# Two layers on one core: where the first loads stand, and how the last three groups' expert tiles are strung together

## The chip, the core and the metric

The kernel runs on one core of a Trainium2 chip, in one launch. The core has TensorE (PE in the profile; its weight loads are PEld), VectorE (DVE), ScalarE (ACT), GpSimd (POOL) and SyncE (SP). Each works through its own queue of instructions in order. DMA transfers are issued from the queues of SP, ACT and POOL. The metric is the device time of one execution in microseconds (us); the median of several runs counts.

## What is computed

Eight sequences of 1024 tokens with 256 channels pass four residual blocks, each `x = x + layernorm(block(layernorm(x)))`: differential attention with 16 heads, a feed-forward block with ternary weights, a gated convolution of 15 taps, and a mixture of 16 experts of which each token takes two.

```python
x = L0_attn_x                                    # (8, 1024, 256)
x = x + _layernorm(_L0_attn_ref(_layernorm(x), ...))
x = x + _layernorm(_L0_ffn_ref(_layernorm(x), ...))
x = x + _layernorm(_L1_attn_ref(_layernorm(x), ...))     # the convolution
x = x + _layernorm(_L1_ffn_ref(_layernorm(x), ...))      # the experts

# attention: two softmax maps per head, the second taken off with a factor lam
lam = exp(sum(lq1 * lk1)) - exp(sum(lq2 * lk2)) + LAM_INIT
comb = a1 - lam[None, :, None, None] * a2
# experts
weights, idx = _gate(xf, gate_w, gate_b)         # two of 16 per token, by groups
h = silu(xf @ We1[e] + be1[e]) * (xf @ We3[e] + be3[e])
y = sum over the two of weights * (h @ We2[e] + be2[e])
z = silu(xf @ ws1 + bs1) * (xf @ ws3 + bs3) @ ws2 + bs2   # for every token
return y + z
```

All of it is in float32.

## The kernel before

Attention (0 to some 2600 us) is an order written out by hand. Time is counted in steps `t` of the pipeline; ten steps make one pair of heads, and `plan` says which helper moves on at which step. The first step is -52, the first score of a maximum comes at step -14 (`LEAD` is 14), the first exponential at step 0. Before any of it stands a setup: the identity, the causal mask and its two halves (`parts`, four copies on SP, L219), the projection weights (loaded on ACT's queue, regrouped by VectorE, L241), WV with each head's mean taken off (L254 to L256), the lam terms (L284 to L296) and 48 rows of biases that TensorE turns into columns (`bias_columns`, L309 to L314). Then each half of a sequence is loaded (`xa`, L340), normalised (L348 to L356), turned by TensorE (L372) and copied to SBUF by ScalarE (L375). Values (L383), keys and queries (L406) follow; a key or query is copied twice by ScalarE and its rest is taken by VectorE (L411 to L414), and SP lays its rows out for the scores (L432). Until the first score these turned tiles and projections share a single PSUM buffer, `pm`.

After the feed-forward block comes the last part, also in an order by hand. For each sequence b there is a convolution (`conv(b)`) and then `gates(b)`: normalisation, the choice of two experts for each token and the shared expert `z`, which goes to DRAM. The sequences form five groups for the experts: groups 0, 1 and 2 of two sequences, groups 3 and 4 of one (sequences 6 and 7). For each group:

- `route` (24 steps with two sequences, 16 with one) counts tokens by expert and gives every token its place in tiles of 128 rows, each tile of one expert. It is mostly VectorE, with some TensorE.
- `expert_tiles` goes through the tiles, 47 for two sequences and 31 for one. In step i it does `outer` of tile i, `tile_product` of i+1, `inner` of i+2, `turn` of i+3, then fetches the weights of tile i+4 (SP, 385 KB, four buffers, L1688) and gathers the tokens of tile i+6 (POOL, an indirect DMA, three buffers, L1676). `turn` is TensorE and ScalarE, `inner` eight TensorE products and two activations (L1708 to L1716), `tile_product` one VectorE product (L1724), `outer` two TensorE products, a copy to one of two `ty` buffers and its store (L1730 to L1733).
- `collected` goes through the group's blocks of 128 tokens: `collect` gathers each token's two expert rows (POOL, `gy`, two buffers each, L1753), loads `z` (`gz`), weights and adds them on VectorE in the next step (L1764), takes the statistics (L1768, L1770), then the power on POOL (L96, L98), then normalises, adds and stores (L1774 to L1777).

`weave` runs several such streams at once: each has a number of steps, and always the one that is least far in proportion moves on. Slot b holds `conv(b)`, `gates(b-1)` and what `slots[b]` names. The part from slot 7 on, with its times in the profile, is:

| stage | us from the start | what is woven |
|---|---|---|
| slot 7 | 3657 to 3784 | conv(7), gates(6), collect of group 1, route(2) and 15 steps of group 2's tiles |
| slot 8 | 3784 to 3905 | gates(7), route(3), the other 38 steps of group 2's tiles |
| group 3 | 3905 to 4025 | 37 steps of its tiles, route(4), collect of group 2 |
| group 4 | 4025 to 4119 | 37 steps of its tiles, collect of group 3 |
| the end | 4119 to 4156 | collect of group 4 |

Of the kernel before, what the change touches and what calls it, by code (L numbers as in the profile page):

```python
# [20 lines left out]
P = 128  # L21
# [6 lines left out]
def kernel(  # L28
# [175 lines left out]
    with ExitStack() as L:  # L204
# [8 lines left out]
        whole = p2.tile([P, 2, P], F32, tag="e", bufs=4, name="whole")  # L213
        make_causal_mask(nc, whole[:, 0, :], mask_val=NEG)
        nc.vector.tensor_copy(whole[:, 1, :], ident)
        parts_ = p2.tile([P, 2, 2, P], F32, tag="e", bufs=4, name="parts")
        for r in range(2):
            for k in range(2):
                nc.sync.dma_start(  # L219
                    parts_[64 * r : 64 * r + 64, :, k, :], whole[64 * k : 64 * k + 64, :, :]  # L220
                )
        masks = wp.tile([P, 2, 2, P], F32R, name="masks")
        nc.vector.tensor_copy(masks, parts_)
# [4 lines left out]
        def pm_tile(name):  # L228
            return ps_m.tile([P, 512], F32, tag="pm", name=name)
# [5 lines left out]
        for m, (wq, wk) in enumerate(((Wq1, Wk1), (Wq2, Wk2))):  # L235
            for w, dst, s in ((wq, WQ, scale), (wk, WK, 1.0)):
                stage = p2.tile([P, ND, D], F32, tag="e", bufs=4, name="stage")
                nc.scalar.dma_start(stage, w.rearrange("(c p) e -> p c e", p=P))
                for dc in range(ND):
                    for hh in range(2):  # L240
                        nc.vector.tensor_scalar_mul(  # L241
                            dst[:, dc, :, :, 2 * hh + m, :].rearrange("p a q d -> p (a q) d"),
                            stage[:, dc, :].rearrange("p (c h d) -> p c h d", h=2, d=HD)[
                                :, :, hh, :
                            ],
                            s,
                        )


        WV = r1.tile([P, ND, H, VD], F32, name="WV")  # L250
        nc.scalar.dma_start(WV.rearrange("p c h v -> p c (h v)"), Wv.rearrange("(c p) e -> p c e", p=P))
        for dc in range(ND):
            vm = small.tile([P, H], F32, tag="hvar", name="vm")
            nc.vector.tensor_reduce(vm, WV[:, dc, :, :], AX.X, ALU.add)  # L254
            nc.vector.tensor_scalar_mul(vm, vm, 1.0 / VD)
            nc.vector.tensor_tensor(  # L256
                WV[:, dc, :, :], WV[:, dc, :, :],
                vm.unsqueeze(2).to_broadcast([P, H, VD]), ALU.subtract,
            )
        WO = q1.tile([P, NHC, D], F32, name="WO")  # L260
        nc.scalar.dma_start(WO, Wo.rearrange("(c p) e -> p c e", p=P))

# [3 lines left out]
        for p in range(2):  # L266
            mine = small.tile([P, 1], F32, tag="mine", name="mine")
            nc.vector.tensor_reduce(
                mine, ident.rearrange("p (h w) -> p h w", h=2)[:, :, 2 * p : 2 * p + 2], AX.XY,
                ALU.add,  # L270
            )
            nc.vector.tensor_scalar(chosen[:, p, :], ones, mine, None, ALU.mult)
            nc.vector.tensor_scalar(
                Ms[p].rearrange("p (n q) -> p n q", q=P),
                ones.unsqueeze(1).to_broadcast([P, NB, P]), 0.0, None, ALU.mult,
            )


        lam_e = []
        for n, (lq, lk) in enumerate(((lq1, lk1), (lq2, lk2))):  # L280
            a = q2.tile([P, H, HD], F32, tag="w2", name="lama")
            c = q2.tile([P, H, HD], F32, tag="w2", name="lamb")
            for t, src in ((a, lq), (c, lk)):
                nc.sync.dma_start(  # L284
                    t.rearrange("p h d -> p (h d)"),
                    src.rearrange("h d -> (h d)").partition_broadcast(P),
                )
            nc.vector.tensor_mul(a, a, c)
            s = p1.tile([P, H], F32, tag="lams", name="lams")
            nc.vector.tensor_reduce(s, a, AX.X, ALU.add)  # L290
            e = p1.tile([P, H], F32, tag=f"lame{n}", name="lame")
            nc.scalar.activation(e, s, AF.Exp)
            lam_e.append(e)
        nlam = const.tile([P, H], F32, name="nlam")
        nc.vector.tensor_sub(nlam, lam_e[1], lam_e[0])
        nc.vector.tensor_scalar_add(nlam, nlam, -LAM_INIT)  # L296

        def bias_columns():
            rows = q2.tile([nrow, P], F32, tag="w2", name="brows")
            at = 0  # L300
            for name, ap in (
                ("f1", fb1.rearrange("(r p) -> r p", p=P)),
                ("c1", cb1.rearrange("(r p) -> r p", p=P)),
                ("e1", be1), ("e3", be3),
                ("s1", bs1.rearrange("(r p) -> r p", p=P)),
                ("s3", bs3.rearrange("(r p) -> r p", p=P)),
            ):
                n = ap.shape[0]
                nc.sync.dma_start(rows[at : at + n, :], ap)  # L309
                col[name] = at  # L310
                at += n
            pt = pm_tile("pt")
            nc.tensor.transpose(pt[:, :nrow], rows, ident[:nrow, :nrow])
            nc.vector.tensor_copy(biasT, pt[:, :nrow])  # L314

# [597 lines left out]
        free_at = total - 2 * NS_ + 2  # L913
        with tc.manual_schedule():
            bias_columns()
            for t in range(min(plan), total + 6):
                if t == free_at:
                    right[1].close()
                    f1 = on_right(2, "ffn_1", 1)

                    F1T = f1.tile([P, ND, FF], F32R, name="F1T")
                    F2T = f1.tile([P, NF, D], F32R, name="F2T")
                    nc.sync.dma_start(F1T.bitcast(F32), f1d)
                    nc.sync.dma_start(F2T.bitcast(F32), f2d)
                step(t)
# [251 lines left out]
    with ExitStack() as L:  # L1177
# [494 lines left out]

        def fetch_tokens(g, i):
            G = groups[g]
            xs = p1.tile([P, D], F32, tag="xs", bufs=3, name="xs")
            nc.gpsimd.indirect_dma_start(  # L1676
                out=xs, out_offset=None, in_=xnd[g],
                in_offset=bass.IndirectOffsetOnAxis(ap=G["token"][:, i : i + 1], axis=0),
                bounds_check=G["blocks"] * P - 1, oob_is_err=False,
            )  # L1680
            tiles[g, i] = [xs]

        def fetch_weights(g, i):
            wt = p1.tile([P, wall.shape[2]], F32, tag="wt", bufs=4, name="wt")
# [50 lines left out]
        def expert_tiles(g):  # L1735
            LT = 2 * groups[g]["blocks"] + E - 1
            stages = (
                (0, outer), (1, tile_product), (2, inner), (3, turn),
                (4, fetch_weights), (6, fetch_tokens),
            )  # L1740
            for i in range(-6, LT):
                for d, stage in stages:
                    if 0 <= i + d < LT:
                        stage(g, i + d)
                yield

        def collect(g, n):

            G = groups[g]
            rows = []  # L1750
            for r in range(2):
                y = p1.tile([P, D], F32, tag=f"gy{r}", bufs=2, name="gy")
# [6 lines left out]
            z = p1.tile([P, D], F32, tag="gz", bufs=4, name="gz")  # L1759
            b, nb = spans[g][0] + n // NB, n % NB  # L1760
            nc.sync.dma_start(z, zd[b * T + nb * P : b * T + (nb + 1) * P, :])
            yield
            for r in range(2):
                nc.vector.scalar_tensor_tensor(  # L1764
                    z, rows[r], G["w"][r][:, n : n + 1], z, ALU.mult, ALU.add
                )
# [12 lines left out]
        def collected(g):  # L1779
# [3 lines left out]
            for k in range(NGB + 3):  # L1783
                for n in range(k - 3, k + 1):
# [23 lines left out]

        def count_route(g):
            return 9 + 8 * spans[g][1]  # L1810

        with tc.manual_schedule():
# [5 lines left out]
            for g, (b0, n) in enumerate(spans[:-2]):  # L1818
                it = chain(lambda g=g: route(g, groups[g]), lambda g=g: expert_tiles(g))
                half = (count_route(g) + count_tiles(g) + 1) // 2  # L1820
                slots[b0 + n + 1].append((it, half))
                slots[b0 + n + 2].append((it, half + 1))
                if b0 + n + 3 <= B:
                    slots[b0 + n + 3].append((later_(collected, g), n * NB + 3))
            for b in range(B + 1):
                streams = []
                after = conv_norm(b + 1) if b + 1 < B else iter(())
                if b < B:
                    streams.append((conv(b, after), 2 * len(windows) + 14))
                if b > 0:  # L1830
                    streams.append((gates(b - 1), 38))
                if b == B:
                    streams.append((later_(route, G0 - 2), count_route(G0 - 2)))
# [3 lines left out]
            weave(  # L1837
                (expert_tiles(G0 - 2), count_tiles(G0 - 2)),
                (route(G0 - 1, groups[G0 - 1]), count_route(G0 - 1)),
                (collected(G0 - 3), spans[G0 - 3][1] * NB + 3),  # L1840
            )
            weave(
                (expert_tiles(G0 - 1), count_tiles(G0 - 1)),
                (collected(G0 - 2), spans[G0 - 2][1] * NB + 3),
            )
# [49 lines left out]
```

## Time and profile before

| what | value |
|---|---|
| median of three runs | 4165.53 us (4164.99 to 4168.62) |
| the profiled execution | 4157.51 us |
| its span, first to last instruction | 4155.8 us |
| mean granted TensorE clock | 0.966 |
| busy: PE, DVE, ACT, POOL | 3770.3, 2820.1, 2307.0, 1475.0 us |

The profile shows the span in 40 equal slices of some 104 us; each digit is the busy share in tenths (PEclk: the granted clock; DMA: the mean share of the 16 DMA engines):

```profile
PE   5998999999999999999999999789999988988764
DVE  5776877876876876886786786688556357374333
ACT  2665666666665665665666666556433543534433
POOL 0222522522431432432342342544311335344465
PEclk9999999999999999999999999899999999999878
DMA  2223232232332233232232222300001655637787
```

The feed-forward block fills slices 26 to 28, the convolutions begin in slice 29, and expert tiles run from slice 32 on.

### The profile page before, as it was taken

The numbers are of one execution on the slowest core, as the hardware profiler recorded it, in microseconds if no ns is written. First come the engines' busy times: TensorE is split into PE (matmuls) and PEld (weight loads), VectorE is DVE, ScalarE is ACT, GpSimd is POOL, SyncE is SP. The second block draws the span as 40 slices with busy tenths as digits, with TensorE's granted clock in tenths as the row PEclk, the third lists the DMA queues.
The fourth block names the chain that finished last, engine by engine and source line by source line (L and its number), as shares of the span: only waits on it lengthen the run. The fifth ranks groups of instructions, "written<-read, shape, count | busy, mean of one in ns | idle before, by whom it ended". The sixth has DMA issues, their size and how long they took to land.

```text
span 4155.8 us, 81449 instructions
## 1 busy us (share of the span) xinstructions
PE 3770.3 (91%) x28903; PEld 2338.5 (56%) x28903; DVE 2820.1 (68%) x6122; ACT 2307.0 (56%) x3870; POOL 1475.0 (35%) x2500
## 2 busy tenths in 40 slices
PE   5998999999999999999999999789999988988764
PEld 2554555554554554554554555578666766766553
DVE  5776877876876876886786786688556357374333
ACT  2665666666665665665666666556433543534433
POOL 0222522522431432432342342544311335344465
PEclk9999999999999999999999999899999999999878
DMA  2223232232332233232232222300001655637787
GB/s 83 65 68 66 68 90 54 69 90 58 75 83 65 66 81 75 57 84 59 61 81 62 70 65 65 106 24 1 6 26 43 185 153 162 185 119 225 213 244 220
DMA packets 286023, 381.38 MB, mean 92 GB/s; under 512 B 61362, under 2 KB 182547, under 8 KB 285364
## 3 DMA queue, kind: packets, MB, share of 16 engines
q1 hardware_dynamic: 226964, 292.74, 26.0%
q0 software_dynamic: 16256, 44.23, 3.9%
q10 hardware_dynamic: 42400, 39.21, 3.1%
q8 instruction: 232, 3.80, 0.4%
q14 instruction: 171, 1.40, 0.1%
HBM read 175.00 MB, written 70.66 MB: 59 GB/s over the span
## 4 chain that ended last, share of the span: by engine, by line
PE 64%; DVE 10%; SPq 8%; DMA 7%; ACT 4%; issue 4%; POOL 2%; ACTq 0%; POOLq 0%; DVEq 0%
PE acc L788 10%; PE sc L751 9%; PE sc L705 6%; SPq L432 6%; PE sc L759 5%; PE pq L406 5%; PE ph L1708 3%; PE pv L383 3%; PE ph L1532 2%; ACT e L766 2%; PE ph L1297 2%; DMA wt<-wall 2%; PE ya L515 2%; PE sc L695 2%; PE py L1085 2%
## 5 line engine op out<-in xcount | busy, mean ns | idle before, releaser
L766 ACT ACTIVATE e<-sc 128x1024 f32<-128x1024 f32 (+1 forms) x1280 | 1194.5, 939 | 554.3 <-PE sc L759 524.4
L723 DVE TENSOR_REDUCE nmx<-sc 128x2 f32<-128x1024 f32 (+3 forms) x1280 | 1108.2, 900 | 343.1 <-PE sc L705 337.4
L769 POOL TENSOR_SCALAR_AFFINE_SELECT e<-e 128x256 f32<-128x256 f32 x1024 | 409.9, 414 | 873.8 <-ACT e L766 865.7
L751 PEld LDWEIGHTS sc<-Q,K 64*128 64x128 f32 x3072 | 288.9, 184 | 682.0 <-issue 490.3
L751 PE MATMUL sc<-Q,K 64*128 64x512 f32 (+3 forms) x3072 | 649.8, 428 | 25.1 <-DVE nmx L723 20.6
L788 PE MATMUL acc<-e,V 128*32 128x512 f32 (+3 forms) x6144 | 631.3, 497 | 0.1
L759 PE MATMUL sc<-M,chosen 64*128 64x512 f32 (+3 forms) x3072 | 531.6, 342 | 11.5 <-DMA M<-mt 11.5
L705 PE MATMUL sc<-K,Q 64*128 64x128 f32 (+3 forms) x4608 | 510.9, 300 | 22.0 <-ACT e L766 15.8
L715 DVE TENSOR_REDUCE nmx<-sc 128x8 f32<-128x1024 f32 x256 | 313.2, 1224 | 204.3 <-PE sc L705 201.5
L705 PEld LDWEIGHTS sc<-K,Q 64*128 64x128 f32 x4608 | 366.8, 186 | 101.7 <-ACT e L766 58.0
L98 POOL TENSOR_TENSOR rstd<-ve,nhalf 128x1 f32<-128x1 f32 (+3 forms) x352 | 394.8, 1121 | 29.3
L1676 POOL DMA_INDIRECT xs<-xnd,r_token x203 | 209.6, 1032 | 346.0 <-PE pt L1695 275.8
L822 POOL TENSOR_TENSOR O<-op 128x124 f32<-128x124 f32 x256 | 123.5, 503 | 563.5 <-DVE op L817 530.1
L1708 PE MATMUL ph<-xT,wt 128*128 128x128 f32 x1624 | 245.0, 298 | 83.6 <-DMA wt<-wall 50.0
L759 PEld LDWEIGHTS sc<-M,chosen 64*128 64x128 f32 x3072 | 293.6, 187 | 13.2 <-DMA M<-mt 11.8
L1708 PEld LDWEIGHTS ph<-xT,wt 128*128 128x128 f32 x1624 | 221.9, 206 | 135.3 <-ACT xT L1699 58.1
L1724 DVE TENSOR_TENSOR thT<-th 128x128 f32<-128x128 f32 x203 | 58.4, 290 | 244.7 <-ACT th L1716 220.9
L788 PEld LDWEIGHTS acc<-e,V 128*32 128x32 f32 x6144 | 130.0, 108 | 131.2 <-issue 81.6
L96 POOL TENSOR_SCALAR ve<-armv 128x1 f32<-128x1 f32 (+1 forms) x224 | 57.4, 256 | 347.4 <-DVE armv L1344 151.5
L1713 ACT ACTIVATE th<-ph,wt 128x128 f32<-128x128 f32 x203 | 74.6, 368 | 180.1 <-PE ph L1708 127.6
L411 ACT COPY raw<-pq 128x512 f32<-128x512 f32 (+1 forms) x160 | 80.2, 501 | 161.4 <-PE pq L406 145.3
L1753 POOL DMA_INDIRECT gy<-yd,r_posu x128 | 134.7, 1052 | 83.6 <-DMA yd<-ty 47.9
(276 smaller groups left out, 6378.3 us busy)
## 6 DMA issues: line engine op xcount, KB each, us to landing
wt<-wall SPq DMA_DIRECT2D x203, 385.0 KB
K<-KC SPq DMA_DIRECT2D x1024, 64.0 KB
Q<-QC SPq DMA_DIRECT2D x1024, 64.0 KB
yd<-ty ACTq DMA_DIRECT2D x203, 128.0 KB
xa<-in_L_attn_x_dram SPq DMA_DIRECT2D x16, 512.0 KB
M<-mt SPq DMA_DIRECT2D x512, 4.0 KB
xr<-in_L_attn_x_dram SPq DMA_DIRECT2D x64, 128.0 KB
x<-xr SPq DMA_DIRECT2D x64, 128.0 KB
```

The lines of the kernel that those rows point to most:

```text
L98: nc.gpsimd.tensor_tensor(rstd, ve, nhalf[:, :n], ALU.pow)
L432: nc.sync.dma_start(d[:, s, :], src[rows, half, :].bitcast(F32))
L705: nc.tensor.matmul(sc[:, r, at_ : at_ + w], quad["Q", i // GB][rows, p, (i % GB) * P : (i % GB + 1) * P], quad["K", k0 // TG][rows, p, k0 ...
L715: nc.vector.tensor_reduce(maxima[b, c][0][:, maps, i : i + GB], sc.rearrange("p m (n q) -> p m n q", q=P), AX.X, ALU.max, negate=True,)
L723: nc.vector.tensor_reduce(maxima[b, c][k][:, maps, i if k == 1 else i - GB], sc[:, :, at_ : at_ + w], AX.X, ALU.max, negate=True,)
L751: nc.tensor.matmul(sc[:, r, at_ : at_ + w], quad["K", kb // GB][rows, p, (kb % GB) * P : (kb % GB + 1) * P], quad["Q", g][rows, p, q0:], s ...
L759: nc.tensor.matmul(sc[:, r, at_ : at_ + w], chosen[rows, p, :], quad["M"][rows, qs], start=False, stop=True,)
L766: nc.scalar.activation(e[:, :, :cols], sc[:, :, :cols], AF.Exp)
L769: nc.gpsimd.affine_select(out=sq, in_=sq, compare_op=ALU.is_ge, fill=0.0, base=0, pattern=[[0, 2], [1, P]], channel_multiplier=-1,)
L788: nc.tensor.matmul(acc[32 * r : 32 * r + 32, q0:], Vs[b, kb][:, 2 * c + r // 2, :], es[r // 2][:, r % 2, at_ : at_ + TG - q0], start=(kb = ...
L1676: nc.gpsimd.indirect_dma_start(out=xs, out_offset=None, in_=xnd[g], in_offset=bass.IndirectOffsetOnAxis(ap=G["token"][:, i : i + 1], axis= ...
L1708: nc.tensor.matmul(ph[:, m, :P], wt[:, k : k + P], xT[:, dc * P : (dc + 1) * P], start=(dc == 0), stop=(dc == ND - 1),)
```

## The change

Two parts of the kernel change. At the start, the setup is cut into helpers (`lay_masks`, `attention_weights`, `bias_columns`) that `plan` places among the first steps. The load of xa comes first on SP; weights, masks and lam terms are loaded on ACT's queue, the bias rows at step 0. While `t` is below -14, turned tiles and projections take the three score buffers (`sc`) instead of the one `pm`.

In the last part, the tiles of groups 2, 3 and 4 become one sequence of 109 tiles that begins in slot 7 (24 steps of route(2), then 31 of tiles) and runs on through six weaves; slot 8 is gone. For groups 3 and 4 the weights are fetched six tiles ahead into eight buffers and the tokens eight ahead into eight, the new ones cut from the tiles of sequences 0 to 3, which are done by then (`more_buffers`). The collects of groups 2, 3 and 4 have four `gy` and five `gz` buffers and one step more between the gather and its use.

```diff
         masks = wp.tile([P, 2, 2, P], F32R, name="masks")
-        nc.vector.tensor_copy(masks, parts_)
+        def lay_masks():
+            whole = p2.tile([P, 2, P], F32, tag="e", bufs=4, name="whole")
+            make_causal_mask(nc, whole[:, 0, :], mask_val=NEG)
+            nc.gpsimd.tensor_copy(whole[:, 1, :], ident)
+            parts_ = p2.tile([P, 2, 2, P], F32, tag="e", bufs=4, name="parts")
+            for r in range(2):
+                for k in range(2):
+                    nc.scalar.dma_start(
+                        parts_[64 * r : 64 * r + 64, :, k, :], whole[64 * k : 64 * k + 64, :, :]
+                    )
+            yield
+            nc.vector.tensor_copy(masks, parts_)
+            yield
         def pm_tile(name):
+            if now[0] < -LEAD:
+                return ps_s.tile([P, 2, 512], F32, tag="sc", name="sc")[:, 0, :]
             return ps_m.tile([P, 512], F32, tag="pm", name=name)
+        def attention_weights():
+            nc.scalar.dma_start(
+                WV.rearrange("p c h v -> p c (h v)"), Wv.rearrange("(c p) e -> p c e", p=P)
+            )
...
+            for m, ws in enumerate(((Wk1, Wk2), (Wq1, Wq2))):
+                for w in ws:
+                    stage = p2.tile([P, ND, D], F32, tag="e", bufs=4, name="stage")
+                    nc.scalar.dma_start(stage, w.rearrange("(c p) e -> p c e", p=P))
+                    stages.append(stage)
+            nc.scalar.dma_start(WO, Wo.rearrange("(c p) e -> p c e", p=P))
+            yield
...
+            a, c = (q2.tile([P, 2, H, HD], F32, tag="w2", name="lam") for _ in range(2))
+            for t, srcs in ((a, (lq1, lq2)), (c, (lk1, lk2))):
+                for k, src in enumerate(srcs):
+                    nc.scalar.dma_start(
+                        t[:, k, :, :].rearrange("p h d -> p (h d)"),
+                        src.rearrange("h d -> (h d)").partition_broadcast(P),
+                    )
+            yield
             nc.vector.tensor_mul(a, a, c)
...
+        first = min(plan)
+        prepared = attention_weights()
+        spread(prepared, [(0, s) for s in (first, first + 3, first + 11, first + 12, first + 20, first + 22)])
+        at(0, first + 28, prepared)
+        spread(lay_masks(), [(0, first + 14), (0, first + 18)])
+        spread(bias_columns(), [(0, 0), (0, 3)])
         with tc.manual_schedule():
-            bias_columns()
-            for t in range(min(plan), total + 6):
+            for t in range(first, total + 6):
...
+        def more_buffers():
+            x = [xpool.tile([P, NB * D], F32, tag=f"x{k}", name=f"spare{k}") for k in range(4)]
+            w = wall.shape[2]
+            spare["wt"] = [x[k][:, j * w : (j + 1) * w] for k in (2, 3) for j in range(2)]
+            spare["xs"] = [x[k][:, 2 * w : 2 * w + D] for k in (2, 3)] + [
+                x[1][:, j * D : (j + 1) * D] for j in range(5, NB)
+            ]
+            spare["gz"] = [x[1][:, j * D : (j + 1) * D] for j in range(5)]
+            spare["gy"] = [
+                [x[0][:, (4 * r + j) * D : (4 * r + j + 1) * D] for j in range(4)]
+                for r in range(2)
+            ]
...
-        def expert_tiles(g):
...
+        def expert_tiles(*gs):
+            line = [(g, i) for g in gs for i in range(2 * groups_blocks(g) + E - 1)]
+            ahead = {g: (4, 6) if g < len(spans) - 2 else (6, 8) for g in gs}
+            w = x = 0
+            for i in range(-ahead[gs[0]][1], len(line)):
+                for d, stage in ((0, outer), (1, tile_product), (2, inner), (3, turn)):
+                    if 0 <= i + d < len(line):
+                        stage(*line[i + d])
+                while w < len(line) and w <= i + ahead[line[w][0]][0]:
+                    fetch_weights(*line[w])
+                    w += 1
+                while x < len(line) and x <= i + ahead[line[x][0]][1]:
+                    fetch_tokens(*line[x])
+                    x += 1
                 yield
...
             yield
+            if late:
+                yield
             for r in range(2):
                 nc.vector.scalar_tensor_tensor(
...
+                gs = (g,) if g < G0 - 3 else (g, g + 1, g + 2)
...
+                if g < G0 - 3:
+                    slots[b0 + n + 1].append((it, half))
+                    slots[b0 + n + 2].append((it, half + 1))
+                else:
+                    slots[b0 + n + 1].append((it, count_route(g) + LT(g) - 17))
...
+            gated_, last = gates(B - 1), later_(collected, G0 - 3)
+            weave((it, 14), (gated_, 19), (route(G0 - 2, groups[G0 - 2]), count_route(G0 - 2)))
+            more_buffers()
+            weave((it, 10), (gated_, 9))
+            weave((it, 12), (gated_, 11), (last, 10))
+            weave((it, LT(G0 - 2) - 22), (later_(route, G0 - 1), count_route(G0 - 1)), (last, 10))
+            weave((it, 11))
+            weave((it, LT(G0 - 1)), (later_(collected, G0 - 2), groups_blocks(G0 - 2) + 4))
             for _ in collected(G0 - 1):
                 pass
```

## The prediction

> **What bounds the kernel now.** I read the 40 slices of the page first. TensorE stands at 9 tenths in slices 2 to 25 but one, which is attention; a change there would have to take TensorE work away, and this one takes none. What can give is the first slice, at 5 tenths, and the last five, at 8 to 4, which are the stages from the last convolution on. So I asked for the timeline of the start (start, duration, engine, line, operation):
>
> ```profile
> 8.10 1.27 DVE L254 TENSOR_REDUCE vm<-WV 128x16 f32<-128x512 f32 x2
> 17.07 0.96 SPq L340 DMA_DIRECT2D xa<-in_L_attn_x_dram  x2
> 22.87 1.41 DVE L348 BATCH_NORM_STATS2 lnst<-xa 128x6 f32<-128x256 f32 x4
> 24.19 0.36 DVE L352 BATCH_NORM_AGGREGATE lnmv<-lnst 128x2 f32<-128x6 f32 x4
> 47.84 5.02 SPq L432 DMA_DIRECT2D K<-KC  x8
> 53.93 10.12 SPq L432 DMA_DIRECT2D Q<-QC  x16
> ```
>
> The tokens are asked for at 17.07, behind fourteen other issues on SP, and used at 22.87. From 53.93 SP issues rows of Q and K back to back (0.63 us each), and the chain of waits runs over it up to about 85 us.
>
> Then the windows by engine, cut where the stages change:
>
> ```profile
> core 0: us, PE busy (x) PEld busy (x) DVE busy (x) ACT busy (x) POOL busy (x), PEclk, DMA share, GB/s
> 3524.50:3657.00 132.50, 126.71 (x959) 98.11 (x957) 50.80 (x202) 74.13 (x213) 45.52 (x57) 1.00 0.66 191
> 3657.00:3735.00 78.00, 66.53 (x493) 45.27 (x493) 68.69 (x245) 22.91 (x54) 41.28 (x56) 0.91 0.33 100
> 3735.00:3784.00 49.00, 38.24 (x214) 29.33 (x214) 29.09 (x100) 19.75 (x54) 31.02 (x42) 0.89 0.71 214
> 3784.00:3905.00 121.00, 103.26 (x611) 83.35 (x611) 44.54 (x200) 61.78 (x176) 36.01 (x37) 0.94 0.73 217
> 3905.00:4025.00 120.00, 76.41 (x410) 62.80 (x409) 57.41 (x188) 39.57 (x126) 79.37 (x96) 0.80 0.78 234
> 4025.00:4119.00 94.00, 61.97 (x372) 48.36 (x372) 26.76 (x79) 39.02 (x125) 53.09 (x62) 0.91 0.87 268
> 4119.00:4156.00 37.00, 0.00 (x0) 0.00 (x0) 18.66 (x48) 0.00 (x0) 22.98 (x32) 0.53 0.36 106
> ```
>
> In order: slot 6; slot 7 while route(2) runs; slot 7 with tiles; slot 8; the weave of group 3; that of group 4; the last collect. TensorE is 96% busy in slot 6, 83% in slot 7, 64% and 66% in the two weaves. The waits of those two (first three lines group 3, then group 4) say why:
>
> ```profile
> DVE gz L1764 <- DMA gy<-yd,r_posu: 41.7, 20, 9.3
> PEld py L1730 <- DVE thT L1724: 22.7, 9, 5.2
> PE py L1730 <- DVE thT L1724: 20.5, 10, 4.9
> ...
> PE ph L1708 <- DMA wt<-wall: 15.1, 12, 3.6
> ACT ty L1732 <- DMA yd<-ty: 8.9, 12, 1.7
> ```
>
> In group 3, VectorE waits 41.7 us for gathered rows asked for only one step earlier, the product of the next tile stands behind it, and TensorE behind that. In group 4 it is the weights: asked for when tile i leaves, needed by tile i+4 two steps later. The chain has them in flight for 5 to 6 us:
>
> ```profile
> 4085.07 5.12 DMA yd<-ty
> 4092.05 6.04 DMA wt<-wall
> ```
>
> **The start.** Moved to ACT's queue or later: four lam loads, four mask copies and six bias loads that stand before xa on SP. xa is issued at 0.8. Issue to use is 22.87-17.07 = 5.8 us at most, with other loads in flight, so it lands by 6.6; the statistics take 1.4. On VectorE the six WV operations come next; WV was in use at 8.10 and they take 2.7, so the aggregate runs at 10.9 in place of 24.19: 13.3 earlier. Bounds of the landing: 2.9 us after the issue (the second lamb load in the chain, with less beside it), and 7.7 (three loads of 512 KB at the 200 GB/s that the window from 5 to 10 us shows): 11 to 16 us earlier.
>
> From the aggregate to the first K issue is 23.65 us now. Afterwards the second half's statistics stand behind the sixteen WK/WQ operations (2.5 us), ACT stops for mask copies (four, some 2.4 us as on SP) and for the lam chain (landing 2.94 after the issue, two VectorE operations 1.7, Exp 0.2), while three score buffers in place of one spare TensorE about 0.65 us for each of three copies. I make K 24.5 and Q 29.6 after the aggregate, against 23.65 and 29.74: nothing. The six bias issues land at step 0 in SP's run of K and Q rows: 0.36+0.25+0.32+0.60+0.57 = 2.1 us, 0 if SP's pauses there (115.4 to 120.4 and 126.3 to 129.4) hide them. I charge all. Start: -13.3+2.1 = **-11** (-7 to -16). If ACT's cover goes, up to 5 us come back, as K's cast stands behind Exp.
>
> **Slot 7.** It takes 55 steps of the sequence, not 39: 24 of route(2) as before, then 31 of tiles, not 15. While route runs, 24/55 = 44% of convolution, gates and collect go beside it, not 62%. VectorE sets that part: 68.7 busy, of which 26.4 are route's operations by line; 26.4+42.3*44/62 = 56 at the same density (68.7 of 78) is 64 us. TensorE sets the rest. Of its 66.5 in the first part 11 are route's, so 55.6*18/62 = 16 move behind; with 12.4 already there, 28. Some 26.5 tiles at 2.1 us (62.0/31 = 2.0 in group 4, 2.3 by single lines) add 56: 84, at 93% 90 us. Slot 7: 154, was 127. Bounds: 138 (all TensorE work at slot 6's 96%) to 168 (31 steps at the 3.2 us of slot 8, plus 64).
>
> **Slot 8's part that is left** (24 tile steps, 28 of 38 gate steps, route(3)): TensorE lines sum to 82 for tiles, 37 gates, 5 route, and overlap to 103. Now 24*2.25+27+5 = 86, overlapped by the same 0.83, at slot 8's 85%: 86 us with rounding up (76 to 95).
>
> **The collect of group 2** goes beside 21 tiles, 11 gate steps and route(4). POOL sets it: gathers follow each other at 1.31 us (4122.87 to 4124.18), so 21+32 make 69; sixteen power pairs at 0.9 make 14, gates' two 2.6: 86. VectorE's wait of 41.7 goes, as rows now have two steps and four buffers; what is late next is POOL itself. I take 92 (86 without a gap, 106 at the 81% that POOL has now, spaced the same way).
>
> **The last 39 tiles** with collect(3). Group 4 runs at 2.71 us a tile after its first (4037 to 4118.5). Weights now have four steps and eight buffers. TensorE's floor is 78. Transfers: 385+128+128 KB a tile and 512 KB a block, less six weights and eight tokens fetched before: 26.4 MB at the 294 GB/s of the busiest 50 us (4050 to 4100) is 90. Without gain 106. I take 97, as the stores' two ty buffers still wait (8.9 us now). *DMA: Bandwidth & Descriptors*, Anatomy of one DMA, in the Trainium skill fits a transfer as 2.0 us plus its bytes at 436 GB/s. By that (an estimate) weights land in 2.9 us, inside two steps, look-ahead buys nothing and this part stays at 106; the chain's 5 to 6 us decide against it.
>
> **The last collect**: one power pair less ahead of the last gather: 36, was 36.8.
>
> **Sum.** 154+86+92+97+36 = 465 against 127+121+120+94+36.8 = 498.8: -34. Two drains and fills (about 12 us at 4025 to 4037, as much at 3905) are inside it. With the start -45. The profiled execution is 4157.5 (span 4155.8), so 4112.5; it stands 8.0 under the median of 4165.5, and the runs to come are compared with that: **4121**. Instructions added are few: the identity half of the mask on POOL, the lam operations halved in number; VectorE and POOL have nothing due there.
>
> **Rivals.** *The waits are replaced, not removed.* The ty stores (5.1 in flight, two buffers: 2.75 us a tile) and POOL hold the tail: 164+92+106+106+37 = 505, +6, less the start's 11: 4160. Halfway, at 484.5, 4140. For: 8.9 us of ty waits, 87% DMA share in group 4. Against: those waits come in 12 of 31 tiles, at most 1.7 each. I give the halfway case, 4140, 0.22.
>
> *The start is lost*: the first K waits for lam and masks on ACT and nothing before 85 us counts: 4132. For: SP's back-to-back run. Against: that run begins with K, whose time moves. 0.08.
>
> *Slower: slot 7 takes over group 3's stall.* collect(1) keeps two buffers and one step of lead there; half of it now meets 31 tile steps, and VectorE's wait for rows holds the products, gates and convolution. At group 3's 3.9 us a step (120/31) plus the 28 us of other TensorE work: 64+149 = 213, 59 over my 154: 4180. It decides once a tile step in slot 7 passes 4.3 us (134/31). For: the same code and 9 blocks. Against: a collect step has 8 us there, against 6.3 in group 3, and VectorE waits only 3.0 us for rows in slot 7 now. 0.08.
>
> *It doesn't do what it says*: the spare buffers are slices of four tiles; if a load waits for the whole tile's readers, look-ahead falls to that of now: about 4140, inside the first rival.
>
> **Chances.** Forecast 0.62, rivals 0.22, 0.08, 0.08. A change under 0.2% (8.3 us) can't be told from none. Faster 0.87, same 0.04, slower 0.09, the last with the far end of the first rival. The sums' bounds, 426 to 512, are ends that would have to come all together; 4094 to 4152 leaves out 0.2.
>
> **What would show it.** Right: xa statistics near 7 us, first K rows near 35; slot 7 about 154 long; almost no wait of gz for gy after it; POOL without gaps during collect(2); tiles of group 4 at 2.2 to 2.5 us with hardly a wait for wt. Wrong: ACT idle before Exp for over 5 us, a tile step of slot 7 over 4 us, ty waiting for yd in most tiles.

## The result, and the profile after

| | median (us) | lowest to highest | executions |
|---|---|---|---|
| before, measured beside it | 4165.26 | 4155.22 to 4170.87 | 6 |
| the changed kernel | 4134.26 | 4124.51 to 4144.38 | 6 |

The ratio is 0.9925 with a 95% interval of 0.9908 to 0.9942: 31 us faster, 24 to 38 by the interval. The forecast was 4121 (4094 to 4152). The profiled execution took 4135.6, its span is 4133.9.

The 40 slices of the changed kernel (busy tenths):

```profile
PE   6999999999999999999999999789899998988864
DVE  6776877876876876786787786578656447364454
ACT  2665666666665665665666666556443553534432
POOL 0222422422431432342342342544311345336465
PEclk9999999999999999999999999899999999999988
DMA  3232232232232232232222222300000654647786
```

TensorE's first slice went from 5 to 6 and its third from last from 7 to 8: it is a little denser at both ends of the span. In between no slice of TensorE has moved by more than a tenth.

The timeline of the start (start, duration, engine, line, operation) answers to the rows shown of before:

```profile
0.81 1.00 SPq L359 DMA_DIRECT2D xa<-in_L_attn_x_dram  x2
6.45 1.40 DVE L367 BATCH_NORM_STATS2 lnst<-xa 128x6 f32<-128x256 f32 x4 [5.35 <-DMA xa<-in_L_attn_x_dram]
...
10.82 0.37 DVE L371 BATCH_NORM_AGGREGATE lnmv<-lnst 128x2 f32<-128x6 f32 x4
...
33.87 5.02 SPq L451 DMA_DIRECT2D K<-KC  x8
38.99 6.27 SPq L451 DMA_DIRECT2D Q<-QC  x10
```

The tokens are asked for at 0.81, the aggregate runs at 10.82 in place of 24.19, the first K rows at 33.87 in place of 47.84 and the first Q rows at 38.99 in place of 53.93. The first exponential's matmul starts at 82.0 us; it was 97.0.

The windows by engine, cut at the new stages: slot 7 with route(2), slot 7 with tiles, the first two weaves, the third, the fourth, the fifth, the sixth, the end.

```profile
core 0: us, PE busy (x) PEld busy (x) DVE busy (x) ACT busy (x) POOL busy (x), PEclk, DMA share, GB/s
3655.00:3720.00 65.00, 52.00 (x337) 33.84 (x336) 52.89 (x194) 16.22 (x36) 27.27 (x36) 0.84 0.26 80
3720.00:3818.00 98.00, 80.73 (x567) 63.18 (x565) 48.28 (x162) 45.69 (x133) 60.98 (x79) 0.97 0.81 244
3818.00:3908.50 90.50, 77.98 (x432) 62.38 (x432) 39.21 (x177) 44.44 (x120) 30.43 (x32) 0.91 0.72 211
3908.50:3947.00 38.50, 27.40 (x163) 22.61 (x162) 19.79 (x61) 16.40 (x53) 30.13 (x37) 0.94 0.89 280
3947.00:3997.50 50.50, 30.63 (x147) 26.46 (x146) 37.75 (x129) 11.62 (x38) 38.41 (x49) 0.67 0.78 229
3997.50:4025.00 27.50, 20.84 (x132) 16.42 (x130) 3.01 (x11) 13.40 (x44) 12.21 (x13) 0.95 0.90 281
4025.00:4096.50 71.50, 50.61 (x324) 39.36 (x324) 25.73 (x76) 33.35 (x110) 40.87 (x51) 0.98 0.83 260
4096.50:4134.00 37.50, 0.00 (x0) 0.00 (x0) 18.99 (x48) 0.19 (x1) 23.73 (x32) 0.54 0.41 121
```

From the first matmul of the last convolution to the end it is 478.8 us, where before had 497.5. The waits from 3908 to 4025 (the third to fifth weave; engine, line, what ended the wait: us, times, longest):

```profile
DVE thT L1770 <- ACT th L1762: 40.3, 18, 3.9
ACT ty L1778 <- PE py L1776: 32.4, 11, 7.4
PEld ph L1754 <- ACT xT L1745: 22.9, 20, 3.7
PEld py L1776 <- DVE thT L1770: 16.6, 5, 7.1
```

and from 4025 to 4096:

```profile
DVE thT L1770 <- ACT th L1762: 47.3, 25, 4.0
PEld ph L1754 <- ACT xT L1745: 32.0, 27, 2.9
PE ph L1754 <- ACT xT L1745: 21.1, 26, 2.5
...
ACT ty L1778 <- DMA yd<-ty: 12.0, 11, 2.6
```

VectorE's 41.7 us for gathered rows are gone from the first list, and the weights (15.1 us before) from the second. What TensorE waits for now is ScalarE's copy `xT`, the turned tokens, in nearly every tile. That wait is not new: in before's list of group 4 (4025 to 4119) it stood above the weights,

```profile
PEld ph L1708 <- ACT xT L1699: 18.2, 17, 2.4
...
PE ph L1708 <- DMA wt<-wall: 15.1, 12, 3.6
```

and the working, which took the weights for what holds that group, has no term for it. Between the copies of a group's last tile and the next group's first one lay 16.2 and 15.8 us before; it is 3.2 and 1.6 now. So the drains that the one sequence was to remove are gone. The chain of waits in the last tiles now runs over stores, not weights:

```profile
4058.26 4.77 DMA yd<-ty
...
4069.26 5.02 DMA yd<-ty
...
4074.76 6.06 DMA yd<-ty
```

### The profile page after: what moved, and what is told of

It is laid out like the page before. It is cut to its first block, busy times and chain, and to the rows that moved or that the text cites. A ratio compares the mean times of both kernels' runs of the same rounds, so it can differ in the third digit from the quotient of the medians.

```text
span 4133.9 us, 81440 instructions
## 1 busy us (share of the span) xinstructions
PE 3774.9 (91%) x28903; PEld 2342.3 (57%) x28903; DVE 2820.0 (68%) x6119; ACT 2307.3 (56%) x3869; POOL 1477.9 (36%) x2501
## 4 chain that ended last, share of the span: by engine, by line
PE 66%; DVE 11%; DMA 6%; SPq 6%; ACT 5%; issue 3%; POOL 2%; ACTq 0%; POOLq 0%; DVEq 0%
PE acc L807 11%; PE sc L770 9%; PE sc L724 6%; PE sc L778 5%; SPq L451 5%; PE pq L425 5%; PE ph L1754 3%; ACT e L785 3%; PE ph L1556 2%; PE pv L402 2%; PE ya L534 2%; PE ph L1321 2%; DMA yd<-ty 2%; PE sc L714 2%; PE py L1109 2%
## 5 line engine op out<-in xcount | busy, mean ns | idle before, releaser
L778 PE MATMUL sc<-M,chosen 64*128 64x512 f32 (+3 forms) x3072 | 534.6, 344 | 11.5 <-DMA M<-mt 11.5
L1719 POOL DMA_INDIRECT xs<-xnd,r_token x165 | 170.6, 1034 | 298.8 <-PE pt L1741 249.5
L1754 PE MATMUL ph<-xT,wt 128*128 128x128 f32 x1384 | 203.5, 293 | 60.7 <-ACT xT L1745 40.7
L1754 PEld LDWEIGHTS ph<-xT,wt 128*128 128x128 f32 x1384 | 186.0, 202 | 100.9 <-ACT xT L1745 73.3
L1090 ACT ACTIVATE gl<-ph,biasT 128x512 f32<-128x512 f32 x128 | 88.2, 689 | 110.1 <-PE ph L1083 69.8
L1321 PE MATMUL ph<-C1s,cxT 128*128 128x512 f32 x288 | 143.9, 624 | 3.0 <-DVE y L1123 3.0
```

Source lines behind the costliest of these rows:

```text
L778: nc.tensor.matmul(sc[:, r, at_ : at_ + w], chosen[rows, p, :], quad["M"][rows, qs], start=False, stop=True,)
L1321: nc.tensor.matmul(pf, xnT[:, dc, i0 : i0 + P], C1s[:, dc, :], start=(dc == 0), stop=False)
L1754: nc.tensor.matmul(ph[:, m, :P], wt[:, k : k + P], xT[:, dc * P : (dc + 1) * P], start=(dc == 0), stop=(dc == ND - 1),)
```

## The experiments

The stage times below are read from each profile: from the first matmul of the last convolution to the copy of tile 24 of the sequence (slot 7), of tile 48 (the next two weaves), of tile 69 (two weaves), of the last tile (39 tiles), and to the end. Single executions of one program differ by 10 to 20 us over the whole span, so a few us between two profiles are read only together with the timed runs. Ratios are against before on the same chip.

### The halves alone

One kernel has the new start and the old last part, another (run twice) the old start and the new last part.

```diff
-            weave((it, 14), (gated_, 19), (route(G0 - 2, groups[G0 - 2]), count_route(G0 - 2)))
...
+            weave(
+                (expert_tiles(G0 - 2), count_tiles(G0 - 2)),
+                (route(G0 - 1, groups[G0 - 1]), count_route(G0 - 1)),
+                (collected(G0 - 3), spans[G0 - 3][1] * NB + 3),
+            )
```

New start only. 

> The new start with the old last part. My theory: the time gained before the first score (15 us earlier at the first exponential of the profile) is passed on by everything behind it, so the median falls by 11 to 15 us, to about 4152. Rival: attention takes it back later, as the profile of the changed kernel stands only 3 us ahead when the last convolution begins; then the median falls by 5 us at most, to 4160 or more.

Measured: 4158.60 against 4170.04, ratio 0.9970 (0.9958 to 0.9981), 12 us.

New last part only. 

> The old start with the new last part. My theory: the last part alone is worth what the two profiles show from the last convolution on, 498.8 against some 479 us, so the median falls by about 19 us, to 4146. Rival (the start gives nothing): the whole 31 us are here, 4134.

Measured: 4162.68 against 4170.04, ratio 0.9979 (0.9967 to 0.9991), 9 us. Less than I had expected, so it was run again, on another chip, after the whole kernel had been repeated:

> The old start with the new last part once more. The whole change gave 31 and 27 us in two comparisons, the new start alone 12.5, this half alone 8.7 (3.8 to 13.8). If the halves add up, this run shows 14 to 20 us (ratio 0.9952 to 0.9966) and the first one was a low draw; if it shows under 11 us again, the halves are worth some 8 us more together than apart.

Measured: 4163.63 against 4178.97, ratio 0.9965 (0.9952 to 0.9979), 15 us.

> The changed kernel once more, beside the next three on one chip. Alone, the new start gave about 12.5 us and the new last part about 8.7, 21 together; the whole gave 31 in its first comparison. If the two parts add up, this run is 19 to 25 us faster than before and the 31 was a good draw; if each part is worth more with the other, it is again 28 us or more faster.

Measured: the whole again, 4142.58 against 4169.60, ratio 0.9933 (0.9919 to 0.9948), 27 us.

So the start is worth 12 us, the last part 9 to 15, the whole 27 to 31. The sum of the halves (21 to 27) meets the whole within the intervals; that they are worth more together isn't shown. The start's term of 11 holds. The last part's 34 doesn't. No kernel has the one sequence without the longer look-ahead and the later collects, so what the sequence is worth by itself isn't measured.

### A third buffer for the stores

```diff
-            y = p1.tile([P, D], F32, tag="ty", bufs=2, name="ty")
+            y = p1.tile([P, D], F32, tag="ty", bufs=3, name="ty")
```

> The changed kernel with three buffers for the expert rows on their way to DRAM instead of two. My theory: stores are a small part of the waits, 0 to 3 us off. Rival (the stores took the place of the weights as what paces the last 39 tiles): 8 us or more off, and the waits of ty for yd gone.

Measured: 4140.90, ratio 0.9931 (0.9914 to 0.9948); the changed kernel has 0.9925 and 0.9933. Nothing. `ty`'s waits for stores are down to 1.3 us there (4016 to 4092), and the last 39 tiles still take 102.0 us. By itself this says that the stores set no pace; further on, that reading turns out to be too quick.

### The old look-ahead

```diff
-            ahead = {g: (4, 6) if g < len(spans) - 2 else (6, 8) for g in gs}
+            ahead = {g: (4, 6) for g in gs}
```

Weights and tokens also go back to four and three buffers.

> The changed kernel with weights fetched four and tokens six tiles ahead and four and three buffers for all groups, the sequence and the collects as changed. My theory: the last 39 tiles go back to 2.7 us each, 6 to 10 us more in all. Rival (weights land inside two steps, by the fit of the Trainium skill's page DMA: Bandwidth & Descriptors, Anatomy of one DMA, an estimate): no change.

Measured: 4148.97, ratio 0.9945 (0.9925 to 0.9965), 21 us under before; the last 39 tiles take 106.9 and the two weaves ahead of them 96.0 (98.9 and 89.1 in the changed kernel). By the medians on this chip it is 8 us above the kernel with the third store buffer, which is level with the changed one. The intervals overlap; the ratios put the look-ahead at 5 to 8 us, and the stages point the same way. The last 39 tiles took 98.9 to 105.0 us in the five profiles that have this part as in the changed kernel, so their share of it is hardly clear of the scatter. By the fit in the Trainium skill, *DMA: Bandwidth & Descriptors*, Anatomy of one DMA, it would have been worth nothing (an estimate). The page gives that fit for one transfer issued by GpSimd, though, and the weights are issued by SP. Before's chain had one of them 6.04 us in flight beside other transfers, where the estimate was 2.9.

### Tile steps moved out of slot 7

```diff
-                    slots[b0 + n + 1].append((it, count_route(g) + LT(g) - 17))
+                    slots[b0 + n + 1].append((it, count_route(g) + LT(g) - 33))
...
-            weave((it, 14), (gated_, 19), (route(G0 - 2, groups[G0 - 2]), count_route(G0 - 2)))
+            weave((it, 30), (gated_, 19), (route(G0 - 2, groups[G0 - 2]), count_route(G0 - 2)))
```

> Sixteen tile steps of group 2 move from slot 7 into the weave after it (30 steps there instead of 14). My theory of the term that I made too small: a tile step costs 2.2 to 2.5 us of TensorE and its pipeline wherever it stands, so slot 7 falls by 33 to 40 us (162 to about 125), the next weave grows by as much, and the total stays within 5 us of the changed kernel. Rival: slot 7 itself is overloaded (the collect of group 1 with its one step of lead stalls VectorE between the tile steps); then the total falls by 6 to 12 us.

Measured: 4144.23, ratio 0.9941 (0.9924 to 0.9958), beside 0.9933 for the changed kernel on that chip. From the last convolution to tile 48 it takes 253.5 us in this kernel, and 253.1 and 246.9 in the two profiles of the changed one. Moving sixteen steps out gains nothing, so slot 7 has no stall that a tile step would escape in the next weave.

### The collects without the change

```diff
-            rows, late = [], g >= len(spans) - 3
+            rows, late = [], False
```

> The last three groups' collects go back to two buffers and one step of lead for the gathered rows; the one sequence and the look-ahead stay. Theory: VectorE's wait for gathered rows comes back while group 2 is collected (20 to 40 us of waits where the changed kernel has next to none), the stretch with it grows from 89 to 97-108 us, and the total is 8 to 20 us above the changed kernel. Rival: it was the longer row of tiles beside the collect that hid the wait, not the buffers; the total stays within 4 us.

Measured: 4146.97, ratio 0.9945 (0.9929 to 0.9962), 4 us above the changed kernel on that chip, with overlapping intervals. Its waits from 3916 to 4005, with group 2's collect, bring VectorE's wait back:

```profile
PEld py L1776 <- DVE thT L1770: 23.9, 8, 6.7
DVE gz L1826 <- DMA gy<-yd,r_posu: 23.2, 17, 4.0
```

Yet this stretch takes 88.1 us, no more than with the buffers (89.1 and 89.9). The wait returned as expected and the time didn't: my theory had the mechanism and not its worth. The timelines of POOL say why. In the changed kernel it goes from one gather or power to the next from 3909.2 to 3993.2 with no gap above 0.31 us; without the buffers it does the same from 3917.1 to 3997.1, with none above 0.41. POOL sets this stretch in both, and VectorE's wait lies in its shadow. Whether the 4 us in all are real stays open.

### The transpose one step earlier

```diff
-                for d, stage in ((0, outer), (1, tile_product), (2, inner), (3, turn)):
+                for d, stage in ((0, outer), (1, tile_product), (2, inner), (4, turn)):
...
-            xT = p1.tile([P, D], F32, tag="xT", bufs=2, name="xT")
+            xT = p1.tile([P, D], F32, tag="xT", bufs=3, name="xT")
```

> The tile's transpose and copy to xT stand one step earlier, with a third xT buffer. Theory: in the last 39 tiles TensorE waits for ScalarE's copy (xT) of the step just before, so the tiles go at 2.5 us with weights long there; with a step more the waits for xT shrink from some 21 us to under 8, the last 39 tiles take 90 to 94 us in place of 99 to 104, and the total is 6 to 15 us below the changed kernel. Rival: transfers at over 80% DMA share or ScalarE's in-order work set the pace; the wait only goes elsewhere (to wt, yd or th) and the total stays within 4 us.

Measured: 4129.68, ratio 0.9913 (0.9896 to 0.9929), 13 us under the changed kernel on the same chip. The wait for `xT` is gone from TensorE's list, but the last 39 tiles still take 101.3 us. The waits from 4017 to 4088 tell why:

```profile
PEld py L1776 <- DVE thT L1770: 26.8, 21, 2.9
ACT ty L1778 <- DMA yd<-ty: 22.7, 15, 2.9
PE py L1776 <- DVE thT L1770: 20.8, 18, 2.6
```

ScalarE stands in `ty` until a store has freed the buffer; Silu, the product `thT` and the last matmul of the next tile are behind it. What this edit gained it gained earlier: tiles 24 to 48, beside the gates, take 83.8 us in place of 90.7 and 89.0. From the last convolution to tile 48 the four kernels with the earlier transpose take 240.1 to 243.1 us, and the seven profiles with the same weaves and the old transpose 246.9 to 254.9. The edit stands in groups 0 and 1 too; from the first convolution to the last these four take 700.2 to 703.5 us and the others 702.7 to 709.1, too close to tell a gain there.

### Both links, and one more

The next kernel adds a third `ty` buffer for groups 3 and 4 to the earlier transpose, cut from the spare rows (`gz` gives up one of five). Another puts product, matmuls and transpose of groups 3 and 4 a further step ahead instead, and a third kernel does both.

```diff
+            spare["ty"] = x[1][:, 4 * D : 5 * D]
...
-            y = p1.tile([P, D], F32, tag="ty", bufs=2, name="ty")
+            if g < len(spans) - 2 or i % 3 < 2:
+                y = p1.tile([P, D], F32, tag="ty", bufs=2, name="ty")
+            else:
+                y = spare["ty"]
```

> The kernel with the transpose one step earlier (13 us below the changed kernel), and a third ty buffer in groups 3 and 4, cut from the spare rows. There ScalarE's copy to ty waits 22.7 us in 15 of the last tiles for the store two tiles before, and with it Silu, the product and py. Theory: that wait is now on the chain; with a third buffer it falls under 8 us and the last 39 tiles go from 101 to 93-97, the total 4 to 8 us lower than with the earlier transpose alone. Rival: as with the third buffer on the changed kernel, nothing changes (within 4 us), since the transfers themselves (DMA share 0.8 to 0.9) set the pace and the wait goes to wt or thT.

Measured: 4122.09 against 4168.70, ratio 0.9880 (0.9861 to 0.9898): 47 us under before by the medians, 50 by the ratio. The waits from 4022 to 4086 have shrunk on both links:

```profile
PEld py L1777 <- DVE thT L1771: 7.4, 9, 1.4
...
ACT ty L1782 <- DMA yd<-ty: 4.9, 4, 2.3
PE ph L1755 <- DMA wt<-wall: 4.4, 3, 1.9
```

For the deeper pipeline:

```diff
+            depth = {g: (1, 2, 4) if g < len(spans) - 2 else (2, 3, 5) for g in gs}
...
+                for k, stage in enumerate((tile_product, inner, turn)):
+                    while c[k] < len(line) and c[k] <= i + depth[line[c[k]][0]][k]:
```

> The kernel with the transpose one step earlier, and in groups 3 and 4 product, matmuls and transpose each one step earlier still (2, 3 and 5 steps ahead of the last product, with a third thT buffer), so that py never needs a product made in the step just before. Theory: py's wait for thT (26.8 us in the last 31 tiles) goes, the last 39 tiles take 92 to 96 in place of 101, the total 4 to 9 us lower than with the earlier transpose alone. Rival: transfers set the pace; weights are used one step sooner, TensorE waits for wt instead, the total stays within 4 us or rises.

Measured: 4129.18, ratio 0.9898 (0.9880 to 0.9916), the last 39 tiles 102.2 us, so no gain over the earlier transpose that the intervals would show. The wait of `py` for `thT` left the list, as expected, and the time stayed: the theory fell. In its place `ty` waits 20.7 us for stores, and `xT`, which ScalarE copies behind it, is late again (24.6 us).

> Both of the two before. Theory of a latency chain (ScalarE and the stores): the gains add, the last 39 tiles reach the transfers' floor that I took (90 to 93), total 8 to 14 us under the kernel with the earlier transpose alone. Rival: the transfers' floor is nearer 100 than 90, and the last 39 tiles stay at 98 to 103 in all three.

Measured: 4122.33, ratio 0.9868 (0.9846 to 0.9889), the last 39 tiles 91.1 us: the third buffer's gain, to which the deeper steps add nothing that can be told. Against the deeper kernel without that buffer, on the same chip, it is 7 us in the medians and 11 in the last 39 tiles.

The window over the last 39 tiles, with the third buffer alone, with the earlier transpose alone, and with both:

```profile
3990.00:4092.00 102.00, 72.93 (x457) 57.28 (x455) 29.05 (x88) 46.02 (x152) 53.39 (x63) 0.95 0.84 262
```

```profile
3986.00:4087.50 101.50, 70.54 (x455) 61.12 (x453) 28.99 (x86) 46.71 (x152) 53.24 (x63) 0.95 0.86 259
```

```profile
3993.50:4084.50 91.00, 70.70 (x454) 61.11 (x453) 28.72 (x86) 46.42 (x152) 54.00 (x63) 0.91 0.92 289
```

The busy times of the engines are the same within 4 us, and 91.0 us at 289 GB/s is 26.3 MB. With either link left the stage takes 101 to 102 us; only without both does it come to the 90 us that the working had as the transfers' floor. That nothing shorter is possible isn't shown: from 4016 to 4050 this kernel moved 304 GB/s. The third store buffer that did nothing is worth 10 us once the link beside it is gone.

## Why the prediction was right, and where it was not

All stages, in us (the old stages don't end at the same tiles, so only the total compares with before's 497.5):

| stage | forecast | changed kernel | again | earlier transpose | with third `ty` too |
|---|---|---|---|---|---|
| slot 7 | 154 | 162.5 | 157.8 | 158.9 | 157.2 |
| next two weaves | 86 | 90.7 | 89.0 | 83.8 | 83.0 |
| two with collect(2) | 92 | 89.1 | 89.9 | 89.9 | 90.0 |
| last 39 tiles | 97 | 98.9 | 102.4 | 101.3 | 91.0 |
| the end | 36 | 37.6 | 37.6 | 37.7 | 37.6 |
| total | 465 | 478.8 | 476.8 | 471.6 | 458.7 |

**The start** came as worked out: xa's statistics at 6.45 (forecast near 7), the aggregate at 10.82 (10.9), from there to K 23.05 us and to Q 28.17 (24.5 and 29.6). 15 us are won at the first exponential. The first eight pairs of heads then take 313.3 us where before took 309.6, and the other profiles of the new start lie at 310.8 to 315.5, those of the old one at 309.4 to 311.3. Over all of attention, from the first exponential to the last, the eleven profiles of the new start take 2516 to 2529 us and the three of the old one 2507 to 2515. So by the profiles part of the 15 us is lost again; but those three were among the faster executions of their kernels, and what makes the difference stays open. The six bias loads do stand in SP's run of rows, as charged (2.1 us), between its K and its Q rows:

```profile
90.14 0.49 SPq L326 DMA_DIRECT2D brows<-in_L_ffn_b_dram  x1
90.69 0.27 SPq L326 DMA_DIRECT2D brows<-in_L_attn_b_dram  x1
91.00 0.78 SPq L326 DMA_DIRECT2D brows<-in_L_ffn_be_dram  x2
91.82 0.57 SPq L326 DMA_DIRECT2D brows<-in_L_ffn_bs_dram  x2
92.49 10.56 SPq L451 DMA_DIRECT2D Q<-QC  x16
```

That time is lost to them was not tried. Timed alone the start gives 12 (8 to 17 by the interval), forecast 11. The rival in which the start is lost falls.

**The collect of group 2** (92, measured 89.1) and **the last collect** (36, 37.6) were right. POOL without gaps, which the prediction named as a sign, is in the trace, and it is what sets this stretch: in the kernel without the buffers 23.2 us of waits for rows came back and the stretch grew by nothing.

**Slot 7 and slot 8's part that is left** are the terms that were mis-sized: 253.1 and 246.9 us together against 154+86 = 240. In slot 7 the TensorE work was put at 84 us and measured 80.7, but the step "at 93% 90 us" failed: TensorE is busy 80.7 of 98, which is 82%. The prediction names no row for its 93%. Its upper bound for slot 7, at the 3.2 us a step of slot 8, adds up to 163 and not 168, and the lower one to some 140 and not 138; the steps did keep slot 8's pace, 31 in 98 us. The tile steps don't stall each other there, as the kernel with shorter slot 7 shows. What was missing, for a good part, is the pipeline's own link: `inner` of a tile needs the `xT` that ScalarE copies in the step before, behind whatever stands in its queue. With the transpose one step earlier the two stages take 242.7 us, with the third `ty` (which begins behind them) 240.1, close to the forecast's sum. They meet it only together: slot 7 stays 3 to 6 us over its 154 in the four kernels with the earlier transpose, which isn't explained, while the other part falls to 82.5 to 85.1.

In that other part the work itself was about right. The profile has 78.0 us of it, where 71 were worked out, at a granted clock of 0.91; one profile of the new last part with the old start has 72.1 us at 0.98 and takes 86.2, as forecast. In the five others with the old transpose it is 74.5 to 78.1 us, at 0.91 to 0.94, and the part takes 87.7 to 91.7.

**The last 39 tiles**: 98.9 and 102.4 against 97 (101.8 to 105.0 in three more kernels with this part as it is). The floor of 90, from 26.4 MB, was good (91.0 once reached, with 26.3 MB). The gap above it was put on the two `ty` buffers, and that is half of it: the store wait and the `xT` wait cover one another, and either alone holds the stage at 101 to 102.

**The rivals.** *The waits are replaced* named 4140 for its halfway case and 484.5 for the last part; the measured 4134 and 478.8 lie nearer to these than to the forecast's 4121 and 465. In full it had 256 in slots 7 and 8 (measured 253.1 and 246.9), 106 for collect(2) (89.1) and 106 for the last tiles (98.9 and 102.4). POOL did not hold collect(2) for longer than I had forecast, so that part fell. The stores hold the last tiles, but only together with `xT`, which neither the forecast nor the rival priced. *Slot 7 takes over group 3's stall* fell: 31 tile steps in 98 us are 3.2 us each, under the 4.3 from which it decides, and VectorE's wait for rows in slot 7 (11.5 us) holds little. *It doesn't do what it says* is unlikely, since taking the look-ahead back cost 5 to 8 us; overlapping intervals leave that short of shown.

The start's sum was right in its mechanism. The last part's wasn't: forecast at 34 us, it gave 9 and 15 when timed alone, and the steps that failed are the 93% of slot 7 and the reading of group 4's waits, which passed over `xT`. That the time still fell inside the range is owed to its width: 4094 to 4152 holds the forecast, the rival's halfway case and the result, and the result lies nearer to the rival. That the kernel with both links cut took 4122, 1 us from the forecast, is luck in part, as it is another kernel with two more edits, timed on another chip; its ratio of 0.9880 (0.9861 to 0.9898) does hold the forecast's 0.9893.

## What to carry to other kernels

A wait that vanishes without gain can mean that another one lies beside it: cut the suspects singly and together before one is called harmless, and give a term to every row of a list of waits, not only to the row that the change is aimed at. In a chain of small steps over four engines, give each hand-over its own term (which queue it stands in, and what stalls that queue), since the busy share of a denser or slower stage doesn't hold for it. And look for a spare buffer where an in-order engine stands for it: here a store held up ScalarE in `ty`, and with it Silu, the product and the last matmul.

## What the runs showed of the hardware that was not expected

TensorE's products slow down in the fourth weave, where route(4) and collect(2) share VectorE and TensorE waits up to 7.1 us at a time. The same matmul of the changed kernel, from 3947 to 3997.5 and from 4025 to 4096 (duration in ns: least, median, greatest):

```profile
L1754 PE MATMUL ph<-xT,spare x40: 270/421/421, 3946.9 to 3994.0; 128*128 128x128 f32 x40
```

```profile
L1754 PE MATMUL ph<-xT,spare x104: 275/275/377, 4027.4 to 4092.1; 128*128 128x128 f32 x104
```

421 ns against 275, at a granted clock of 0.67 against 0.98; the kernel with the earlier transpose shows the same 421. *TensorE: Matmul & The Clock Gate*, HAM oscillation, in the Trainium skill has the clock fall after idle gaps longer than some 3.4 us; this trace agrees with it in its longest gap, 6.9 us before 3961.3, behind which the clock stands at 0.50 (3962 to 3974). It stands at 0.50 from 3984 to 3998 as well, though, and in the 8 us before that no gap is over 0.9 us; what made it fall there stays open. Nine tiles take 50.5 us there, and 44 to 56 in the other versions of the new last part. Moving part of collect(2) into the fifth weave, where POOL is busy 12.2 of 27.5 us, wasn't tried.

The scatter between executions of one program was larger than either half of the change: the new last part with the old start ran from 4150.91 to 4170.19 us in twelve executions on one chip. From the last convolution to the end the old last part takes 497.5 us in the profile of before and 510.6 in that of the new start alone, the same code. The profile of before that the forecast started from lay 8 us under its median. Halves worth 9 to 15 us can't be read from single profiles under such scatter; the repeated runs tell them.
